# Attention plus a non-local block on one core: another order of large and small products in the q and k stages

## The chip, the cores and the metric

The kernel runs on one core of a Trainium2 chip. The metric is the device time of one execution in microseconds (us). A core has a matrix engine (TensorE, "PE" in the profile, with "PEld" for its weight loads), a vector engine (VectorE, "DVE"), a scalar engine (ScalarE, "ACT"), GpSimd ("POOL") and DMA queues. Matmul results land in PSUM, from which ACT or DVE has to read them into SBUF.

## The reference, cut to what matters

Two layers run on x, which is 8 images of 512 channels and 32 x 32 positions, in float32. The change touches only the projections q and k of the first layer.

```python
def _L0_conv_ref(x, Wq, bq, Wk, bk, Wv, bv, Wp, bp):
    q = _conv1x1(x, Wq, bq).reshape(B, h, d, H * W)     # 512x512 weights times 512x1024 data, per image
    k = _conv1x1(x, Wk, bk).reshape(B, h, d, H * W)
    v = _conv1x1(x, Wv, bv).reshape(B, h, d, H * W)
    attn = jax.nn.softmax(jnp.einsum('bhdn,bhdm->bhnm', q, k) * scale, axis=-1)
    out = jnp.einsum('bhnm,bhdm->bhdn', attn, v).reshape(B, C, H, W)
    return x + _conv1x1(out, Wp, bp)
# layer 1: theta, phi, g, a 256x256 product, the output projection, batch normalization
```

## The kernel before

Every 1x1 convolution is one step of Strassen's scheme (Winograd's form): 7 products of quarters in place of 8. The weight quarters and their sums are `w[:, 0..6]`, the data quarters are "11", "12", "21", "22" and their sums t1 to t4. In q and k, for the images 1 to 7, three of the seven products are again split into seven small products each, so that a stage has 4 large products (4 matmuls each, 128 x 512 outputs) and 3 x 7 = 21 small ones (one matmul each, 128 x 256 outputs). A float32 matmul appears in the profile as two records.

```python
SEVEN = (("11", 0, "11", 0, (("11", True),)), ("s1t1", 3, "t1", 1, (("22", True),)),
         ("s2t2", 4, "t2", 0, (("12", True),)), ("s4", 6, "22", 1, (("12", False),)),
         ("s3t3", 5, "t3", 0, (("22", False),)), ("12", 1, "21", 2, (("11", False),)),
         ("t4", 2, "t4", 0, (("21", True),)))
# (name, weight index, data, slot, (result quarter, True: write it with the bias / False: add to it))
FOUR = tuple((*one[:4], ()) for one in (SEVEN[0], SEVEN[1], SEVEN[2], FIVE[4]))
#       large products of q and k:     11 (slot 0), s1t1 (slot 1), s2t2 (slot 0), s3t3 (slot 0)
INNER = {"WqT": (1, 6, 2), "WkT": (1, 6, 2), "WpT": (1, 2)}      # which products are split again, in this order
AHEAD = {6: ((0, 0, "11", False),), 9: ((0, 0, "12", False),), 11: ((0, 1, "12", False),)}
BEHIND = {6: ((0, 1, "11", False),), 9: ((1, None, "22", True),), 11: ((1, None, "12", False),),
          15: ((0, None, "22", False), (0, None, "21", False))}
STEPS = {2: [0] * 4 + [1] * 14, 3: [0, 0, 0, 1, 2, 2, 2, 2, 1, 2, 2, 2, 2, 1, 1, 1]}
```

A large slot is a PSUM tile of two banks, one for each half m of the output rows. The three large products of slot 0 accumulate onto each other, and what stands in the slot is read out between them. `STEPS[3]` says how many small products follow each large matmul ("unit") 0 to 15. `AHEAD` and `BEHIND` say after which unit a slot (or its half m) is read, ahead of or behind the small products of that unit.

```python
def nested(name, stage, w, data, tags, first, add):              # yields one small product at a time
    slots, three = [bank(tag, f"{name}_in_{tag}") for tag in tags], len(INNER[stage]) == 3
    goes_to = {1: ("11", "21", False), 6: ("12", "22", False), 2: ("21", "t4", True)}
    for n, (q, di, begins) in enumerate(goes_to[i] for i in INNER[stage]):
        a, d = inner_blocks(w, stage, n), data[f"inner {di}"]
        pair = slots[::-1] if n % 2 else slots
        begun = set()
        for _, wi, di, s, reads in SEVEN:
            ps = pair[s % 2 if s < 2 else 1][:, s // 2, n % 2 * 256:(n % 2 + 1) * 256]
            pe(nc.tensor.matmul(ps, a[wi], d[di], start=s not in begun, stop=True, skip_group_check=True))
            begun.add(s)
            for to, is_first in reads:
                c = rows(q).start + int(to[0]) - 1
                at = cols(q).start + (int(to[1]) - 1) * 256
                (first if is_first and (begins or three) else add)((slice(c, c + 1), slice(at, at + 256)), ps)
            yield
# in seven(), inside the loop over the large matmuls:
                pe(nc.tensor.matmul(to_ps, lhsT(k), rhs(k), start=(s, at) not in begun, stop=(k == nk - 1),
                                    skip_group_check=True))
                read_parts(AHEAD.get(unit, ()))
                for _ in range(next(counts, 0)):
                    next(steps)
                read_parts(BEHIND.get(unit, ()))
                if unit in fills:
                    fills[unit]()
                unit += 1
# `first` in q and k: nc.scalar.activation(..., AF.Identity, bias=...) on ACT, one of 512 for each half, or one of 256
# `add`: nc.vector.tensor_tensor(at, at, ps, ALU.add) on DVE; pinned in program order in q, not in k
# ... cut: one image
            fills = {3: lambda: more_sums(nxt["data"], (3,), dve), 4: lambda: more_sums(nxt["data"], (4,), dve),
                     5: lambda: (of_t4.extend(inner_parts(nxt["data"], "t4", dve)), of_t4[0](), of_t4[1]()),
                     7: lambda: (of_t4[2](), of_t4[3]())}
            q, peak_q = heads_of(b + 1, "q", weights("WqT"), bq, nxt["data"], dve, inner="WqT", later=later, fills=fills)
# ... v of the next image; then k, whose gaps on DVE take the sums t1..t4 of the attention output o:
            fills = {unit: lambda i=i: more_sums(nxt["o"], (i,), dve) for unit, i in ((3, 1), (5, 2), (8, 3), (12, 4))}
```

`PE` runs strictly in the order of the program. With u for the large units and s0 to s20 for the small products, a q or k stage of before is

```
u0 u1 u2 u3 | s0 | u4 | s1 s2 | u5 | s3 s4 | u6 | s5 s6 | u7 | s7 s8 | u8 | s9 | u9 | s10 s11 |
u10 | s12 s13 | u11 | s14 s15 | u12 | s16 s17 | u13 | s18 | u14 | s19 | u15 | s20
large: u0-3 = 11, u4-7 = s1t1, u8-11 = s2t2, u12-15 = s3t3; of each four, the first two are half m = 0
small: s0-6 go to quarter 11, s7-13 to quarter 12, s14-20 to quarter 21; they use two PSUM tiles A and B by turns (s0 A, s1 B, s2 A, ...)
```

Of the kernel before, what the change touches and what calls it, by code (L numbers as in the profile page):

```python
# [30 lines left out]
def unshifted(ctx: ExitStack, tc: tile.TileContext, a: dict, out: bass.AP):  # L31
# [33 lines left out]
    dve = sp = pe  # L65
# [3 lines left out]
    def bank(tag, name):  # L69
        return psum.tile([P, 2, 512], F32, tag=tag, name=name)  # L70
# [40 lines left out]
        queue += (["WqT", "WvT", "WkT"] if b < B - 1 else []) + ["WpT", "tp", "WgT"]  # L111
    loaded = []

    INNER = {"WqT": (1, 6, 2), "WkT": (1, 6, 2), "WpT": (1, 2)}
    WIDTH = 7 * C + 3 * 3 * P
    rest = {}

# [79 lines left out]
    def more_sums(data, which, pin=lambda ins: None):  # L197
        for i in which:
            l, r = {1: ("12", "11"), 2: ("22", "t1"), 3: ("22", "12"), 4: ("21", "t2")}[i]
            data[f"t{i}"] = block(f"t{i}_{data['name']}")  # L200
            pin(nc.vector.tensor_tensor(data[f"t{i}"], data[l], data[r], ALU.subtract))
# [14 lines left out]
    def quarters_of(t):  # L216
# [13 lines left out]

    FOUR = tuple((*one[:4], ()) for one in (SEVEN[0], SEVEN[1], SEVEN[2], FIVE[4]))
    AHEAD = {6: ((0, 0, "11", False),), 9: ((0, 0, "12", False),), 11: ((0, 1, "12", False),)}
    BEHIND = {6: ((0, 1, "11", False),), 9: ((1, None, "22", True),), 11: ((1, None, "12", False),),
              15: ((0, None, "22", False), (0, None, "21", False))}
    STEPS = {2: [0] * 4 + [1] * 14, 3: [0, 0, 0, 1, 2, 2, 2, 2, 1, 2, 2, 2, 2, 1, 1, 1]}

    def nested(name, stage, w, data, tags, first, add):

        slots, three = [bank(tag, f"{name}_in_{tag}") for tag in tags], len(INNER[stage]) == 3
        goes_to = {1: ("11", "21", False), 6: ("12", "22", False), 2: ("21", "t4", True)}
        for n, (q, di, begins) in enumerate(goes_to[i] for i in INNER[stage]):
            a, d = inner_blocks(w, stage, n), data[f"inner {di}"]
# [6 lines that stand above are left out]
                for to, is_first in reads:  # L251
                    c = rows(q).start + int(to[0]) - 1
                    at = cols(q).start + (int(to[1]) - 1) * 256
                    (first if is_first and (begins or three) else add)((slice(c, c + 1), slice(at, at + 256)), ps)
                yield

    def seven(name, w, data, positions_out, first, add, between=None, early=False,
              by_chunk=False, inner=None, fills=()):

        nk, half = w.shape[2], w.shape[3]
        tags = list(free)
        free[:] = [tags[3], tags[1], tags[0], tags[2]] if early else [tags[3], tags[1], tags[2], tags[0]]
        slots, begun = {}, set()
        steps, three = iter(()), inner and len(INNER[inner]) == 3
        unit, counts = 0, iter(STEPS[len(INNER[inner])] if inner else ())
        if inner:
            free[:] = [tags[1], tags[2], tags[3], tags[0]]
            steps = nested(name, inner, w, data, tags[2:], first, add)  # L270

        def read(reads, ps):
            for to, is_first in reads:
                (first if is_first else add)(to, ps)

        def read_parts(parts):
            for s, m, to, is_first in parts if three else ():
                if m is None:
                    read(((to, is_first),), slots[s])
                else:  # L280
                    c = rows(to).start + m
                    read((((slice(c, c + 1), cols(to)), is_first),), slots[s][:, m, :])

        for n, (what, wi, di, s, reads) in enumerate(FOUR if three else FIVE if inner else EARLY if early else SEVEN):
            if s not in slots or early and what == "t4":
                slots[s] = bank(tags[s], f"{name}_{s}_{n}")
                begun -= {one for one in begun if one[0] == s}
            ps, d = slots[s], data[di]
            if positions_out:
                parts = [(ps.rearrange("p h (i f) -> p (h i) f", f=half)[:, i, :], i * half // 512,  # L290
                          lambda k, i=i: d[:, k, i * P:(i + 1) * P], lambda k: w[:, wi, k, :])
                         for i in range(512 // P)]
            else:
                parts = [(ps[:, m, :], m, lambda k, m=m: w[:, wi, k, m * P:(m + 1) * P], lambda k: d[:, k, :])
                         for m in range(half // P)]
            work = [(*part, k) for part in parts for k in range(nk)]
            if by_chunk and n == 0:
                work.sort(key=lambda one: one[4])
            for to_ps, at, lhsT, rhs, k in work:
                pe(nc.tensor.matmul(to_ps, lhsT(k), rhs(k), start=(s, at) not in begun, stop=(k == nk - 1),  # L300
                                    skip_group_check=True))
                begun.add((s, at))
                read_parts(AHEAD.get(unit, ()))
                for _ in range(next(counts, 0)):
                    next(steps)
                read_parts(BEHIND.get(unit, ()))
                if unit in fills:
                    fills[unit]()
                unit += 1
            read(reads, ps)  # L310
            if between and n in between:
                between[n]()

    def rows(q):
        return q[0] if isinstance(q[0], slice) else slice((int(q[0]) - 1) * CC // 2, int(q[0]) * CC // 2)

    def cols(q):
        return q[1] if isinstance(q[1], slice) else slice((int(q[1]) - 1) * 512, int(q[1]) * 512)
# [11 lines left out]
    _, w_first = weights_tile("WqT", C // 2)  # L330
# [474 lines left out]
    for b in range(B):  # L805
        last = b == B - 1
        nxt = {}
# [19 lines left out]
        if not last:  # L827
            inner_sums(nxt["data"], "21", dve)
            later, of_t4 = [], []
            fills = {3: lambda: more_sums(nxt["data"], (3,), dve), 4: lambda: more_sums(nxt["data"], (4,), dve),  # L830
                     5: lambda: (of_t4.extend(inner_parts(nxt["data"], "t4", dve)), of_t4[0](), of_t4[1]()),
                     7: lambda: (of_t4[2](), of_t4[3]())}
            q, peak_q = heads_of(b + 1, "q", weights("WqT"), bq, nxt["data"], dve, inner="WqT",
                                 later=later, fills=fills)
            load_w(nc.sync)

            def norm():
                nxt["products"] = normalize(denominators(next_bank(f"den_{b}")[:, 0, :]))

            v = values(b + 1, weights("WvT"), nxt["data"], {1: norm, 2: lambda: [one() for one in later], 5: lambda: nxt["products"]()})  # L840
            load_w(nc.sync)

            nxt["o"], of_21 = data_sums(quarters_of(o), f"o_{b}", ()), []
            fills = {unit: lambda i=i: more_sums(nxt["o"], (i,), dve) for unit, i in ((3, 1), (5, 2), (8, 3), (12, 4))}
            if b:
                fills[13] = lambda: (of_21.extend(inner_parts(nxt["o"], "21", dve)), of_21[0](), of_21[1]())
                fills[14] = lambda: (of_21[2](), of_21[3]())
            later_k = []
            k, peak_k = heads_of(b + 1, "k", weights("WkT"), bk, nxt["data"], later=later_k, inner="WkT",
                                 fills=fills)  # L850
            if b:
                inner_sums(nxt["o"], "t4", dve)
            load_w(nc.sync)
        else:
            nonlocal_(b - 1, held["x"], nxt["data"], held["f"], weights("WgT"), lambda: None,
                      {3: lambda: nxt.update(d=denominators(next_bank(f"den_{b}_1")[:, 0, :]))})
            z[b - 1] = [held["x"][:, cc, :] for cc in range(CC)]
            between = {4: late_unit(b - 1, 0, sums_now=False)}
            normalize(nxt["d"])()
            load_w(nc.sync)  # L860
            put_away(b - 1)
            for i, tag in enumerate("vqk"):
                reload(i, mats, tag)
            reload(3, foldp, "fold")
# [258 lines left out]
```

## Time and profile before

| | |
|---|---|
| time, median of 3 | 2166.21 us (2166.19 to 2167.51) |
| span of the profiled execution | 2164.1 us, mean granted TensorE clock 0.996 |
| one image in the steady part | 265.9 us (start of q at 721.92 to start of q at 987.80) |
| q stage | 23.62 us (987.80 to 1011.42) |
| k stage | 24.33 us (1036.80 to 1061.13) |
| DVE adds of 128x256, 128x512, 128x1024 out of PSUM | about 0.42, 0.69, 1.22 us each |
| ACT writes with bias of 128x256, 128x512 | 0.474, 0.684 us each |

The page of the profile gives each engine's busy time, the chain of work that ended last, and groups of instructions. The chain of a window, in order of time, shows for each stretch which instruction the end had to wait for: an unbroken row of PE pieces means that nothing held the matrix engine. The timeline lists one engine's instructions by their starts. The ends of matmuls are modelled, so a distance is taken from start to start.

### The profile page before, as it was taken

What the parts mean: (1) busy time and instruction counts of PE and PEld (TensorE: products, weight loads), DVE (VectorE), ACT (ScalarE), POOL (GpSimd) and SP (SyncE); (2) the same over time, 40 slices, a digit from 0 to 9 for tenths busy, and PEclk for the clock granted to TensorE, in tenths of its full rate; (3) what the DMA queues carried; (4) which work ended last, traced back from release to release, by engine and by line L of the source; (5) the groups of instructions that cost most, each with busy time, mean ns of one, the idle gap of its engine ahead of it and who ended that gap; (6) DMA issues with size and microseconds to landing.
All of it is one profiled execution on the core that took longest, in us unless ns stands there. A gap on an engine that the chain in (4) does not pass through costs nothing.

```text
span 2164.1 us, 30088 instructions
## 1 busy us (share of the span) xinstructions
PE 2133.4 (99%) x12510; PEld 1119.4 (52%) x12510; DVE 1395.0 (64%) x1634; ACT 762.1 (35%) x910; POOL 205.5 (9%) x256
## 2 busy tenths in 40 slices
PE   9999999999999999999999999999999999999996
PEld 4534664356733567335663366633666346743462
DVE  6466756667576665766657666576674675756736
ACT  1464104641046310463105621066212652056106
POOL 0111100110001100011000100011000110001000
PEclk9999999999999999999999999999999999999998
DMA  6333444333143331433323342233434234122658
GB/s 220 137 48 63 136 155 127 49 80 116 72 129 50 77 115 72 132 50 85 105 98 110 50 99 93 99 106 50 107 133 155 41 46 138 51 58 39 221 200 339
DMA packets 53375, 229.97 MB, mean 106 GB/s; under 512 B 9712, under 2 KB 16112, under 8 KB 45680
## 3 DMA queue, kind: packets, MB, share of 16 engines
q1 hardware_dynamic: 41552, 198.21, 27.2%
q0 software_dynamic: 10192, 28.46, 10.9%
q8 instruction: 100, 1.64, 0.3%
q10 hardware_dynamic: 1488, 1.32, 0.2%
q14 instruction: 43, 0.35, 0.1%
HBM read 140.79 MB, written 46.27 MB: 86 GB/s over the span
## 4 chain that ended last, share of the span: by engine, by line
PE 95%; ACT 2%; DVE 1%; DMA 1%; issue 0%; SPq 0%; DVEq 0%; ACTq 0%
PE ps L460 20%; PE po L486 20%; PE pv L300 9%; PE ptp L300 9%; PE pp L300 7%; PE pq L300 5%; PE pk L300 5%; PE pg L300 4%; PE pk_in_s L249 3%; PE pq_in_s L249 3%; PE pf L626 3%; PE pz L300 2%; PE pp_in_s L249 2%; PE pwf L661 1%; ACT z L777 1%; PE den L432 0%
## 5 line engine op out<-in xcount | busy, mean ns | idle before, releaser
L463 ACT ACTIVATE e<-ps 128x1024 f32<-128x1024 f32 x512 | 523.0, 1025 | 426.1 <-PE ps L460 420.6
L469 DVE TENSOR_TENSOR acc<-acc,e 128x1024 f32<-128x1024 f32 x384 | 470.0, 1224 | 144.3 <-ACT e L463 140.7
L486 PE MATMUL po<-e,v 64*64 64x512 f32 x4096 | 528.7, 589 | 0.7 <-ACT w_WgT L628 0.7
L460 PE MATMUL ps<-q,k 64*64 64x512 f32 x4096 | 529.1, 589 | 0.0
L486 PEld LDWEIGHTS po<-e,v 64*64 64x64 f32 x4096 | 156.4, 133 | 283.5 <-issue 275.8
L460 PEld LDWEIGHTS ps<-q,k 64*64 64x64 f32 x4096 | 155.4, 133 | 284.2 <-issue 275.1
L499 POOL DMA_DIRECT2D fold<-acc x189 | 147.1, 778 | 984.1 <-DMA fold<-acc 638.5
L467 DVE TENSOR_TENSOR acc<-e,e 128x1024 f32<-128x1024 f32 x64 | 78.3, 1224 | 144.0 <-ACT e L463 144.0
L649 ACT ACTIVATE g<-pg,gb 128x512 f32<-128x512 f32 x31 | 21.3, 688 | 374.2 <-PE pg L300 374.1
L300 PE MATMUL pv<-w_WvT,t_x 128*128 128x256 f32 x512 | 116.4, 381 | 0.0
L300 PE MATMUL ptp<-w_tp,t_x 128*128 128x256 f32 x512 | 114.4, 379 | 0.0
L300 PEld LDWEIGHTS pv<-w_WvT,t_x 128*128 128x128 f32 x512 | 96.6, 190 | 18.5 <-issue 5.7
L300 PEld LDWEIGHTS ptp<-w_tp,t_x 128*128 128x128 f32 x512 | 97.3, 190 | 13.2
L300 PE MATMUL pq<-t_x,w_WqT 128*128 128x512 f32 x200 | 101.4, 600 | 1.1 <-DVE w_WqT L788 0.8
L300 PE MATMUL pk<-t_x,w_WkT 128*128 128x512 f32 x200 | 101.5, 599 | 0.0
L300 PE MATMUL pp<-t_o,w_WpT 128*128 128x512 f32 x208 | 100.8, 592 | 0.0
L427 POOL TENSOR_SCALAR q<-q,gates 128x1024 f32<-128x1024 f32 x32 | 35.3, 1114 | 690.3 <-DVE gates L425 595.2
L415 ACT COPY v<-pv 128x1024 f32<-128x1024 f32 x32 | 32.4, 1012 | 173.2 <-PE pv L300 173.2
L300 PE MATMUL ptp<-w_tp,x 128*128 128x256 f32 x384 | 87.4, 381 | 0.0
L300 PE MATMUL pv<-w_WvT,x 128*128 128x256 f32 x384 | 86.8, 379 | 0.0
L383 ACT ACTIVATE k<-pk_in_s,bk 128x256 f32<-128x256 f32 x84 | 38.9, 474 | 116.1 <-PE pk_in_s L249 116.1
L383 ACT ACTIVATE q<-pq_in_s,bq 128x256 f32<-128x256 f32 x84 | 38.7, 474 | 115.2 <-PE pq_in_s L249 115.2
(179 smaller groups left out, 2333.6 us busy)
## 6 DMA issues: line engine op xcount, KB each, us to landing
fold<-acc POOLq DMA_DIRECT2D x189, 128.0 KB, 3.1
w_WqT<-kept_WqT SPq DMA_DIRECT2D x7, 2368.0 KB, 8.9
w_WkT<-kept_WkT SPq DMA_DIRECT2D x7, 2368.0 KB, 9.2
r<-den_d SPq DMA_DIRECT2D x32, 512.0 KB, 7.4
x<-in_x_dram SPq DMA_DIRECT2D x31, 512.0 KB, 6.3
w_WpT<-kept_WpT SPq DMA_DIRECT2D x6, 2176.0 KB, 8.4
w_WvT<-kept_WvT SPq DMA_DIRECT2D x7, 1792.0 KB, 7.1
w_tp<-kept_tp SPq DMA_DIRECT2D x7, 1792.0 KB, 7.8
```

What stands on the lines that cost most here:

```text
L249: pe(nc.tensor.matmul(ps, a[wi], d[di], start=s not in begun, stop=True, skip_group_check=True))
L300: pe(nc.tensor.matmul(to_ps, lhsT(k), rhs(k), start=(s, at) not in begun, stop=(k == nk - 1), skip_group_check=True))
L383: nc.scalar.activation(t[:, c, q[1]], ps, AF.Identity, bias=bias[:, c:c + 1])
L415: seven(f"pv_{b}", w, data, True, lambda q, ps: nc.scalar.copy(at(q), as_v(ps)), lambda q, ps: dve(nc.vector.tensor_tensor(at(q), at(q), a ...
L427: nc.gpsimd.tensor_scalar(q[:, p, :], q[:, p, :], gate[:, p:p + 1], 1.0, ALU.mult, ALU.mult)
L460: pe(nc.tensor.matmul(ps[c * P // 2:(c + 1) * P // 2, j, :], k[r, p, keys], q[r, p, h * 512:(h + 1) * 512], start=True, stop=True, skip_gr ...
L463: nc.scalar.activation(e, ps, AF.Exp, scale=SCALE)
L467: nc.vector.tensor_tensor(accs[u], es[u, 0], e, ALU.add)
L469: ins = nc.vector.tensor_tensor(accs[u], accs[u], e, ALU.add)
L486: pe(nc.tensor.matmul(ps[j * D:(j + 1) * D, r, :], v[keys, m, (2 * p + j) * D:(2 * p + j + 1) * D], e[keys, j, :], start=(m == 0), stop=(m ...
L499: nc.gpsimd.dma_start(to, part_of, accum_op=ALU.add)
L626: pe(nc.tensor.matmul(ps[:, c, :], tp[:, i, c * P:(c + 1) * P], tp[:, i, CI:], start=(i == 0), stop=(i == NB - 1)))
```

## The change

In q and k the second large product, s1t1, comes in two halves, one before and one behind the third, s2t2. A slot is now always read as a whole, and what is read of it begins a quarter of the result where it can: the reads of 11 and of 12 become writes with bias on ACT, and the small products of the quarters 11 and 12 are then all added on DVE. The small products are taken in the order quarter 11, quarter 21, quarter 12. The counts of small products behind the units 4 and 8 change from 2 and 1 to 1 and 2, and the sums on DVE that fill the gaps sit behind other units. What it is for: fewer and larger reads of the large slots, and no read of one half while the other is being written.

```diff
-    INNER = {"WqT": (1, 6, 2), "WkT": (1, 6, 2), "WpT": (1, 2)}
+    INNER = {"WqT": (1, 2, 6), "WkT": (1, 2, 6), "WpT": (1, 2)}
...
-    AHEAD = {6: ((0, 0, "11", False),), 9: ((0, 0, "12", False),), 11: ((0, 1, "12", False),)}
-    BEHIND = {6: ((0, 1, "11", False),), 9: ((1, None, "22", True),), 11: ((1, None, "12", False),),
-              15: ((0, None, "22", False), (0, None, "21", False))}
-    STEPS = {2: [0] * 4 + [1] * 14, 3: [0, 0, 0, 1, 2, 2, 2, 2, 1, 2, 2, 2, 2, 1, 1, 1]}
+    HALVES = ((0, 0), (0, 1), (1, 0), (2, 0), (2, 1), (1, 1), (3, 0), (3, 1))
+    STEPS = {2: [0] * 4 + [1] * 14, 3: [0, 0, 0, 1, 1, 2, 2, 2, 2, 2, 2, 2, 2, 1, 1, 1]}
+    READS = {3: ((0, "11", True),), 9: ((0, "12", True),), 11: ((1, "22", True), (1, "12", False)),
+             15: ((0, "22", False), (0, "21", False))}
...
-                    (first if is_first and (begins or three) else add)((slice(c, c + 1), slice(at, at + 256)), ps)
+                    (first if is_first and begins else add)((slice(c, c + 1), slice(at, at + 256)), ps)
...
-        for n, (what, wi, di, s, reads) in enumerate(FOUR if three else FIVE if inner else EARLY if early else SEVEN):
+        products = FOUR if three else FIVE if inner else EARLY if early else SEVEN
+        for n, m in HALVES if three else ((n, None) for n in range(len(products))):
+            what, wi, di, s, reads = products[n]
...
-            work = [(*part, k) for part in parts for k in range(nk)]
+            work = [(*part, k) for part in (parts if m is None else parts[m:m + 1]) for k in range(nk)]
...
-                read_parts(AHEAD.get(unit, ()))
-                for _ in range(next(counts, 0)):
-                    next(steps)
-                read_parts(BEHIND.get(unit, ()))
+                for ahead in (True, False):
+                    for one, to, is_first in READS.get(unit, ()) if three and ahead == (unit < 15) else ():
+                        read(((to, is_first),), slots[one])
+                    for _ in range(next(counts, 0) if ahead else 0):
+                        next(steps)
...
-            fills = {3: lambda: more_sums(nxt["data"], (3,), dve), 4: lambda: more_sums(nxt["data"], (4,), dve),
-                     5: lambda: (of_t4.extend(inner_parts(nxt["data"], "t4", dve)), of_t4[0](), of_t4[1]()),
-                     7: lambda: (of_t4[2](), of_t4[3]())}
+            fills = {4: lambda: more_sums(nxt["data"], (3,), dve),
+                     5: lambda: (more_sums(nxt["data"], (4,), dve), of_t4.extend(inner_parts(nxt["data"], "t4", dve))),
+                     6: lambda: (of_t4[0](), of_t4[1]()), 7: lambda: (of_t4[2](), of_t4[3]())}
...
-            fills = {unit: lambda i=i: more_sums(nxt["o"], (i,), dve) for unit, i in ((3, 1), (5, 2), (8, 3), (12, 4))}
+            fills = {unit: lambda i=i: more_sums(nxt["o"], (i,), dve) for unit, i in ((5, 1), (7, 2), (11, 3), (12, 4))}
```

The order on PE after the change, in the same notation:

```
u0 u1 u2 u3 | s0 | u4 | s1 | u5 | s2 s3 | u6 | s4 s5 | u7 | s6 s7 | u8 | s8 s9 | u9 | s10 s11 |
u10 | s12 s13 | u11 | s14 s15 | u12 | s16 s17 | u13 | s18 | u14 | s19 | u15 | s20
large: u0-3 = 11, u4-5 = s1t1 half 0, u6-9 = s2t2, u10-11 = s1t1 half 1, u12-15 = s3t3
small: s0-6 go to quarter 11, s7-13 to quarter 21, s14-20 to quarter 12; tiles A and B by turns as before
slot 0 is read whole behind u3, u9 and u15, slot 1 behind u11
```

More of the change, by code (lines that the diff above doesn't have):

```diff
@@ L233, in unshifted @@
     FOUR = tuple((*one[:4], ()) for one in (SEVEN[0], SEVEN[1], SEVEN[2], FIVE[4]))
-    AHEAD = {6: ((0, 0, "11", False),), 9: ((0, 0, "12", False),), 11: ((0, 1, "12", False),)}
-    BEHIND = {6: ((0, 1, "11", False),), 9: ((1, None, "22", True),), 11: ((1, None, "12", False),),
-              15: ((0, None, "22", False), (0, None, "21", False))}
-    STEPS = {2: [0] * 4 + [1] * 14, 3: [0, 0, 0, 1, 2, 2, 2, 2, 1, 2, 2, 2, 2, 1, 1, 1]}
+    HALVES = ((0, 0), (0, 1), (1, 0), (2, 0), (2, 1), (1, 1), (3, 0), (3, 1))
+    STEPS = {2: [0] * 4 + [1] * 14, 3: [0, 0, 0, 1, 1, 2, 2, 2, 2, 2, 2, 2, 2, 1, 1, 1]}
+    READS = {3: ((0, "11", True),), 9: ((0, "12", True),), 11: ((1, "22", True), (1, "12", False)),
+             15: ((0, "22", False), (0, "21", False))}
     def nested(name, stage, w, data, tags, first, add):
-        slots, three = [bank(tag, f"{name}_in_{tag}") for tag in tags], len(INNER[stage]) == 3
+        slots = [bank(tag, f"{name}_in_{tag}") for tag in tags]
         goes_to = {1: ("11", "21", False), 6: ("12", "22", False), 2: ("21", "t4", True)}
@@ L274, in read @@
                 (first if is_first else add)(to, ps)
[L276 to L282, printed above, removed]
-        for n, (what, wi, di, s, reads) in enumerate(FOUR if three else FIVE if inner else EARLY if early else SEVEN):
+        products = FOUR if three else FIVE if inner else EARLY if early else SEVEN
+        for n, m in HALVES if three else ((n, None) for n in range(len(products))):
+            what, wi, di, s, reads = products[n]
             if s not in slots or early and what == "t4":
```

## The prediction, made before the changed kernel was run

> **What bounds the kernel now.** First the page: busy time by engine, and the granted clock.
>
> ```profile
> span 2164.1 us, 30088 instructions
> PE 2133.4 (99%) x12510; PEld 1119.4 (52%) x12510; DVE 1395.0 (64%) x1634; ACT 762.1 (35%) x910; POOL 205.5 (9%) x256
> ...
> PEclk9999999999999999999999999999999999999998
> ```
>
> The matrix engine has work for the whole span, at full clock; DVE and ACT have a third and two thirds of theirs free. The change neither adds nor removes a matmul, so it can only win time in which PE stood still, or lose some. Busy shares cannot show that, so I read, second, the chain of work that ended last, in the window of one k stage (columns: start, length, what).
>
> ```profile
> 779.08 0.88 PE pk_in_s L249 x4
> 779.96 0.02 issue
> 779.99 0.48 ACT k L383
> 780.47 0.02 issue
> 780.49 0.04 DVE k L323
> 780.53 0.57 issue
> 781.10 0.43 DVE k L323
> 781.52 0.04 issue
> 781.57 1.13 PE pk_in_s L249 x4
> ...
> 785.71 1.11 PE pk L300 x2
> ...
> 789.41 1.11 PE pk L300 x2
> ```
>
> Undisturbed, four records of a small pair take 0.86 and two records of a large matmul 0.86 (both stand in most rows of the chain). So s7 waited from 779.94 to 781.57 and its pair then took 0.27 too long: the wait is for the DVE add of s5, which came last in DVE's queue. The two rows of 1.11 are u10 and u12, 0.25 too long each. The same view of q has no gap, only three pieces that are too long:
>
> ```profile
> 732.00 0.98 PE pq_in_s L249 x4
> ...
> 736.00 1.11 PE pq L300 x2
> ...
> 739.69 1.11 PE pq L300 x2
> ```
>
> Third, the timeline around u10 in another q stage, of which I show the DVE add, PE's weight load, its matmul and the next small one:
>
> ```profile
> 1001.12 0.69 DVE L323 TENSOR_TENSOR q<-q,pq 128x512 f32<-128x512 f32 x1 [2.17 <-PE pq L300]
> ...
> 1001.86 0.30 PEld L300 LDWEIGHTS pq<-t_x,w_WqT 128*128 128x128 f32 x2 [0.39 <-DVE q L323]
> 1001.86 1.12 PE L300 MATMUL pq<-t_x,w_WqT 128*128 128x512 f32 x2
> ...
> 1002.83 0.38 PE L249 MATMUL pq_in_s<-x,w_WqT 128*128 128x256 f32 x1
> ```
>
> The add of 1001.12 reads half 0 of slot 0; u10 writes half 1, the other bank. It still starts only 0.05 behind the add's end at 1001.81, so a write waits for every earlier read of its slot, whichever half. The load then no longer hides: u10 ends at 1002.83, 0.97 after its start instead of 0.86. So a late reader that ends at R lets PE run from R + 0.16.
>
> **What these waits cost in all.** A stage has 16 large matmuls and 21 small ones. Large: 3.43 us for the first four of k, 0.858 each; small: 0.43 each. 16 x 0.858 + 21 x 0.43 = 22.75. A k stage takes 24.33, so 1.58 is lost (1.08 at s7, 0.25 each at u10 and u12). A q stage takes 23.62; its first row is 3.63 instead of 3.43 (the turn from attention, which stays), so 0.62 to 0.67 is lost at the three places. With seven stages of each kind the most that can be won is 7 x (0.62 + 1.58) = **15.4 us**, 0.7% of 2166.2.
>
> **What the Trainium skill says.** "TensorE: Matmul & The Clock Gate", step-by-step list of Part 2: weight loads are pulled ahead, so that the next tile's load lies under the current matmul. The trace agrees: loads of 0.19 cost nothing in the rows of 0.86, and 0.11 where a wait held the load. "PSUM — Partial Sum Buffer", section on bank collisions: guard PSUM by bank. The two halves are two banks, so a guard by bank would have let u10 go; here the wait covers the whole slot, and the trace decides. "VectorE: DVE Perf Modes", section on the TRN2 errata: a fixed cost for each instruction, so small operands pay more. The trace agrees: DVE adds back to back start every 0.34, 0.59 and 1.13 us for 256, 512 and 1024 columns, which is about 0.08 plus 0.26 for each 256.
>
> **The change part by part.**
>
> *Reads.* Before, a stage has 9 small, 4 half and 3 whole adds on DVE: 9 x 0.34 + 4 x 0.59 + 3 x 1.13 = 8.8 us; after, 17 small and 3 whole: 9.2. ACT had 12 small and 2 half writes and now has 4 and 6. In a stage of 23 us neither engine becomes the bound by its sum. What counts is when each read ends.
>
> *Large slots.* Slot 0 is read by ACT behind u3 and u9. The two writes take 0.59 + 0.68 from 0.27 after the unit (an ACT or DVE read starts some 0.2 to 0.3 after the end of its product), so they end 1.54 after it. The next writers of slot 0, u6 and u12, come 3.4 and 4.3 later. Slot 1 is not written again after its read. **The waits at u10 and u12 go**: 0.5 in each stage.
>
> *Small products.* A and B alternate, so s(i+2) waits for the read of s(i). With "small, small, large" repeated there are 1.29 us between the end of s(i) and the start of s(i+2); the read needs 0.27 + 0.42 + 0.16 = 0.85. Slack: 0.44, while one of the filling sums or whole adds on DVE is 1.13. So I followed DVE's queue in its new order, times from the start of u0 (u0 held by 0.11 as in q).
>
> - DVE is busy with older work until 4.4 in q (before's t3 starts at 992.13, q at 987.73), 2.5 in k.
> - s0's add follows ACT's write: 4.54 to 4.96. s1's: 5.54 to 5.96. Then in q the sum t3 until 7.0, the adds of s2 and s3 until 7.77, t4 until 8.8, the adds of s4 and s5 until 9.24 and 9.58. The writers s2 to s7 come at 6.13, 6.56, 7.85, 8.28, 9.57, 10.00; each is free 0.1 or more earlier. The narrowest are s6, 0.17, and s7, 0.26. In k a single sum stands here (until 8.7), with the adds of s4 and s5 done by 9.15 and 9.49. **The wait at s7 goes**: 0.12 in q, 1.08 in k.
> - s8 to s13 (four of them read by ACT) have 0.4 and more, s13 0.44.
> - Behind u11 (its end 16.45) DVE starts the whole add from slot 1 at 16.72, until 17.85. s14's add comes behind it and ends at 18.27; s16 wants to start at 18.17 and gets 18.43. **A new wait of 0.26** in each stage.
> - In k two sums follow, so s16's add ends at 20.08 and s18 loses another **0.09**. In q nothing.
>
> *Sum.* q: 0.62 removed, 0.26 added: 0.36 won. k: 1.58 removed, 0.35 added: 1.23 won. 7 x (0.36 + 1.23) = **11.1 us**, so 2166.2 - 11.1 = 2155.1.
>
> **The rivals.** *All waits vanish.* If the whole add behind u11 gets behind s14's add, or a DVE read starts 0.2 instead of 0.27 after its product, the 0.26 goes: 2166.2 - 15.4 = 2150.8. For it: 0.2 is seen for some adds. Against it: in q the adds are pinned in the order of the program.
>
> *The wait moves to the chain of small adds.* Now 17 of 21 small products need DVE, and in k the adds are not pinned, so the order is open; already in the trace of before, the add of s5 lands behind two half adds that the program has one on each side of it. If a sum of 1.13 gets ahead of a waited-for add at two places in each stage, each costs 1.13 - 0.44 = 0.7, and 14 x 1.4 = 19.6 takes back the whole gain: 2166.2 - 15.4 + 19.6 = 2170. For it: the slack of 0.44 is less than one sum. Against it: PE's program order and the new places of the sums look chosen for it.
>
> *DVE hands its backlog on.* The later sums of o leave DVE busy about 4.4 us into the output projection instead of the 3.7 of before (1064.70 against its start at 1060.97). That stage has one small product between large ones and takes 23.21 against 20 x 0.858 + 14 x 0.43 = 23.18, so it waits for nothing now, and DVE idles there for 0.75 soon after. A loss of 0.5 in each of six such stages would give 2158.
>
> **Range and chances.** The lower end is the first rival, all waits gone, and a little: 2150. The upper end stands some two thirds of the way from 2155 to the second rival's 2170: 2164. Over 2% is 43 us: the gain is capped at 15.4, and a loss of that size needs 3.1 us in each of 14 stages, which only a quite different order of instructions would make. So faster by over 2%: 0.01; within 2%: 0.97; slower by over 2%: 0.02.
>
> **What would show it right or wrong.** In the chain of q and k, the rows of 1.11 at u10 and u12 and k's gap before s7 should be gone; k should take about 23.1 us and q 23.25; the pair with s16 should be some 0.26 too long, with its load waiting for a DVE add. The group of 128x256 DVE adds should grow from 63 to 119 for q and for k, and the 128x512 adds vanish there. I am wrong if PE loads wait for DVE at several small products, if the projection behind k grows past 23.21, or if k stays above 24.

## The result and the profile after

The changed kernel takes 2176.11 us (2175.83 to 2176.69) against 2166.20 for the kernel before: 9.9 us slower, ratio 1.0045 with a 95% interval of 1.0028 to 1.0062. The prediction was 2155.1, with a range of 2150 to 2164: its direction was wrong as well as its size. First the page again, busy time by engine:

```profile
span 2174.1 us, 30056 instructions
PE 2129.2 (98%) x12510; PEld 1120.5 (52%) x12510; DVE 1399.6 (64%) x1690; ACT 746.5 (34%) x854; POOL 205.1 (9%) x256
...
PEclk9999999999999999999999999999999999999998
```

The count of matmuls and the clock are as before and the span is 10 us longer, so PE now stands still more. The instruction counts moved as the prediction worked out: the group of small DVE adds is 119 for q (7 stages of 17), from 63.

```profile
L319 DVE TENSOR_TENSOR q<-q,pq_in_s 128x256 f32<-128x256 f32 x119 | 48.3, 419 | 49.1 <-PE pq_in_s L250 46.0
```

The chain of work that ended last, in a q stage (start, length, what):

```profile
735.56 0.93 PE pq_in_s L250 x4
...
741.66 0.87 PE pq L295 x2
742.53 0.02 issue
742.55 1.27 ACT q L386 x2
743.83 0.02 issue
743.85 1.23 DVE q L319
...
745.18 0.43 DVE q L319
745.61 0.04 issue
745.65 1.13 PE pq_in_s L250 x4
```

What the change was meant to remove is gone. No piece at the large units is longer than 0.87 and the old wait at s7 is 0.07 in this stage (the row of 0.93) and gone in the next (0.87); in k the row of s6 and s7 is 0.86. But s16, due at 742.53 + 0.86 + 0.86 = 744.25 (s14 and s15, then u12), starts at 745.65, and its pair takes 0.27 too long: a new wait of **1.67 us**. The chain names it link by link: u11 ends, ACT writes quarter 22 from slot 1 in two pieces, and only then does DVE's whole add from slot 1 start, then the add of s14, then s16. The timeline gives the same, with what each waited for in brackets:

```profile
742.35 0.59 PE L250 MATMUL pq_in_s<-x,w_WqT 128*128 128x256 f32 x2
...
742.55 1.27 ACT L386 ACTIVATE q<-pq,bq 128x512 f32<-128x512 f32 x2 [0.39 <-PE pq L295]
...
743.85 1.22 DVE L319 TENSOR_TENSOR q<-q,pq 128x1024 f32<-128x1024 f32 x1 [2.17 <-ACT q L386]
745.18 0.75 DVE L319 TENSOR_TENSOR q<-q,pq_in_s 128x256 f32<-128x256 f32 x2
...
745.65 0.70 PE L250 MATMUL pq_in_s<-i_x,w_WqT 128*128 128x256 f32 x2 [1.42 <-DVE q L319]
```

DVE stood idle for 2.17 us ahead of its add: it was not overloaded, it was held, at the end by ACT. In the k stage the add starts 1.32 behind u11 as well. By stage, from the chain's pieces, q went from 23.62 to 24.69 and k from 24.33 to 24.56 (one q stage of each kernel is 0.35 longer, and the first k stage went from 25.12 to 26.63). Summed over the seven of each: q 7.5, k 2.9, together 10.4 us. The spans differ by 10.0, because the last output projection got 0.48 shorter (24.62 to 24.14).

### The profile page after: what moved, and what is told of

Same layout as the page of the kernel before. It is cut to its first block, busy times and chain, and to the rows that moved or that the text cites. A ratio compares the mean times of both kernels' runs of the same rounds, so it can differ in the third digit from the quotient of the medians.

```text
span 2174.1 us, 30056 instructions
## 1 busy us (share of the span) xinstructions
PE 2129.2 (98%) x12510; PEld 1120.5 (52%) x12510; DVE 1399.6 (64%) x1690; ACT 746.5 (34%) x854; POOL 205.1 (9%) x256
## 3 DMA queue, kind: packets, MB, share of 16 engines
q10 hardware_dynamic: 1488, 1.32, 0.2%
## 4 chain that ended last, share of the span: by engine, by line
PE 94%; ACT 2%; DVE 2%; DMA 1%; issue 0%; ACTq 0%; DVEq 0%
PE ps L456 20%; PE po L482 20%; PE pv L295 9%; PE ptp L295 9%; PE pp L295 7%; PE pk L295 5%; PE pq L295 5%; PE pg L295 4%; PE pq_in_s L250 3%; PE pk_in_s L250 3%; PE pf L622 3%; PE pz L295 2%; PE pp_in_s L250 2%; PE pwf L657 1%; ACT z L773 1%; DVE k L319 1%
## 5 line engine op out<-in xcount | busy, mean ns | idle before, releaser
L319 DVE TENSOR_TENSOR q<-q,pq_in_s 128x256 f32<-128x256 f32 x119 | 48.3, 419 | 49.1 <-PE pq_in_s L250 46.0
L295 PEld LDWEIGHTS ptp<-w_tp,x 128*128 128x128 f32 x384 | 72.4, 190 | 13.0 <-issue 3.6
```

Of the source, the lines that this page charges most:

```text
L319: pin(nc.vector.tensor_tensor(at, at, ps if len(ps.shape) == 3 else ps.unsqueeze(1), ALU.add))
```

## The experiments

Theory A: the program lets no DVE read of a PSUM slot run beside an ACT read of it, so the two kinds of reads from slot 1, which the change puts side by side behind u11, run one behind the other. Theory B: 17 small adds are more than DVE can return in time, in whatever order. Theory C: DVE waits because ACT writes to the same SBUF tile, q or k.

**The add ahead of the writes.**

```diff
-             READS = {... 11: ((1, "22", True), (1, "12", False)), ...}
+             READS = {... 11: ((1, "12", False), (1, "22", True)), ...}
```

> The changed kernel with one edit: behind u11 the whole add from slot 1 (to quarter 12, on DVE) comes ahead of ACT's two writes from slot 1 (quarter 22). Theory A (DVE may not read a PSUM slot while ACT reads it, so the add waits 1.3 us for ACT's two writes and s16 waits for the add's follower): the add starts 0.2 to 0.3 us after u11 instead of 1.3, the wait at s16 shrinks from 1.68 to about 0.3 us, and the time falls by about 14 x 1.3 = 18 to 2156 to 2159 us. Theory B (17 small adds in a row are too many for DVE, whatever the order): the wait at s16 stays over 1 us and the time over 2172.

Measured: 2159.37 us (2158.95 to 2159.64), ratio to the kernel before 0.9968 (0.9955 to 0.9980). One exchange of two reads wins 16.7 us over the changed kernel. The chain in q:

```profile
737.18 0.87 PE pq L295 x2
...
738.15 1.23 DVE q L319
...
739.48 0.43 DVE q L319
739.91 0.04 issue
739.95 1.13 PE pq_in_s L250 x4
```

The timeline of the two readers:

```profile
738.15 1.22 DVE L319 TENSOR_TENSOR q<-q,pq 128x1024 f32<-128x1024 f32 x1 [0.94 <-PE pq L295]
...
739.40 1.26 ACT L386 ACTIVATE q<-pq,bq 128x512 f32<-128x512 f32 x2 [1.71 <-DVE q L319]
```

The add starts 0.10 behind u11 instead of 1.32, both by the chain, which counts from the modelled end of the product. DVE's idle time ahead of it falls from 2.17 to 0.94, and s16 loses 0.18 + 0.27 = 0.45 instead of 1.67. ACT now waits for DVE instead (its writes start at 739.40, where the add has ended), but nothing waits for ACT there. Each stage is shorter by 1.23 (q 23.46, k 23.33), and 14 x 1.23 = 17.2. Theory B falls: DVE has as many adds as in the changed kernel. The loss of 0.45 at s16 is 0.15 over the expected 0.3, and the time lies just over the expected range, for a reason told below.

**ACT's reads of slot 1 into a tile of their own.**

```diff
+                        if (one, to) == (1, "22"):
+                            first(to, data["11"])                # quarter 22 begun from a piece of x
+                            for hh in range(2):                  # slot 1 still read, into a tile nobody reads
+                                nc.scalar.activation(aside, slots[one][:, hh, :], AF.Identity, bias=...)
```

> The changed kernel, but ACT's two reads of slot 1 behind u11 write to a tile of their own that nothing reads, and quarter 22 is begun by ACT from a piece of x instead, early in the stage (so slot 1 is left out of quarter 22). Theory A (the reads of the PSUM slot exclude each other): DVE's add to quarter 12 still starts only about 1.3 us after u11, and the time stays within 3 us of 2176. Theory C (the add waits because ACT writes the same SBUF tile q or k): the add starts 0.2 to 0.3 us after u11 and the time falls to about 2158.

Measured: 10151.44 us. This kernel leaves slot 1 out of quarter 22, and the piece of x made q and k so large that the kernel's bound on the scores sent it through its second branch too, so its time can't be compared. Its q stages, ahead of that branch, already show the add only when ACT has done (ACT's reads from 743.73, the add at 745.16). The next run takes the second branch away.

> As the run with the aside tile, but ACT begins quarter 22 early with the bias alone (the piece of x times zero), so that q and k stay small and only the first branch of the kernel runs; slot 1 is still left out of quarter 22, and ACT still reads slot 1 behind u11, into a tile that nothing reads. Theory A (reads of one PSUM slot exclude each other): DVE's add to quarter 12 starts about 1.3 us after u11, the wait at s16 is about 1.7 us, the time 2173 to 2179. Theory C (the wait comes from ACT's write to q or k): the add starts 0.1 to 0.3 us after u11, the time is 2158 to 2162.

```diff
-                            first(to, data["11"])
+                            first(to, data["11"], 0.0)           # scale 0: the bias alone
```

Measured: 2179.26 us (one run; the kernel before beside it 2166.40). That is just over the expected 2173 to 2179. The timeline of DVE and ACT:

```profile
743.43 1.41 ACT L306 ACTIVATE aside<-pq,bq 128x512 bf16<-128x512 f32 x2 [0.39 <-PE pq L295]
...
744.88 1.22 DVE L325 TENSOR_TENSOR q<-q,pq 128x1024 f32<-128x1024 f32 x1 [2.31 <-ACT aside L306]
```

ACT's writes to quarter 22 were over at 726.5, so at this point ACT and DVE share nothing but slot 1, which both only read, and the add still waits until ACT is done, 1.45 behind the start of its first read. Theory C falls. (A stage takes 0.1 to 0.2 more than in the changed kernel: ACT's two writes to the one small tile take 1.41 instead of 1.27.)

Nor do ACT and DVE keep apart whenever both read PSUM. In the changed kernel, behind u9, a DVE add from the small tiles and an ACT write from slot 0 run side by side:

```profile
739.61 0.78 DVE L319 TENSOR_TENSOR q<-q,pq_in_s 128x256 f32<-128x256 f32 x2 [2.18 <-PE pq_in_s L250]
739.69 0.68 ACT L386 ACTIVATE q<-pq,bq 128x512 f32<-128x512 f32 x1
```

It is the common tile that makes one wait for the other.

**The add cut in halves, one bank each.**

```diff
+                        if (one, to) == (1, "12"):
+                            for hh in range(2):
+                                c = rows(to).start + hh
+                                read((((slice(c, c + 1), cols(to)), False),), slots[one][:, hh, :])
+                            continue
```

> The changed kernel with the add from slot 1 cut in two halves, each reading one bank of the slot; ACT's two writes stay ahead and read one bank each. If reads exclude each other bank by bank: the first half add starts about 0.9 us after u11, when ACT is done with its first half, and the wait at s16 shrinks by about 0.5 us, the time by 5 to 8 us. If they exclude each other by the whole slot, as the writes before did: the first half add starts 1.3 us after u11 as the whole add did, and the time stays within 2 us of 2176.

Measured: 2174.62 us (one run), within the 2 us expected for the whole slot. The timeline:

```profile
742.74 1.26 ACT L391 ACTIVATE q<-pq,bq 128x512 f32<-128x512 f32 x2 [0.39 <-PE pq L295]
...
744.03 1.29 DVE L324 TENSOR_TENSOR q<-q,pq 128x512 f32<-128x512 f32 x2 [2.17 <-ACT q L391]
```

The first half add reads only bank 0, which ACT finishes with at about 743.4, and it starts at 744.03, when both of ACT's reads are over. So this program keeps the two readers apart by slot (the tile), not by bank.

**The add behind the adds of s14 and s15, and the sums of o moved.**

```diff
-             READS = {... 11: ((1, "22", True), (1, "12", False)), ...}
+             READS = {... 11: ((1, "22", True),), ...}
+    BACK = {11: ((1, "12", False),)}                             # read behind the small products of the unit
-    ... for unit, i in ((5, 1), (7, 2), (11, 3), (12, 4))}      # k: sums t1..t4 of o
+    ... for unit, i in ((5, 1), (7, 2), (8, 3), (9, 4))}
```

> The changed kernel with the whole add from slot 1 placed behind the adds of s14 and s15, ACT's writes from slot 1 left where they are, and in k the third and fourth sum of o behind the units 8 and 9 instead of 11 and 12. Theory A: s16 finds the add of s14 done, no wait of over 0.1 us is left in q or k of the images 2 to 7, each stage takes about 22.9 us (q) and 22.8 (k), and the time is 2150 to 2154 us, 12 to 16 below the kernel before. Theory B: waits at s16 or s18 of 0.3 us or more stay, and the time is over 2160.

Measured: 2152.66 us (2152.33 to 2153.09), ratio to the kernel before 0.9936 (0.9919 to 0.9952): faster than both. A q stage takes 23.05, a k stage 22.85, and the chain in k has only PE pieces, of which the one with s18 is 0.05 too long:

```profile
786.22 0.86 PE pk_in_s L251 x4
787.08 0.86 PE pk L296 x2
787.94 0.48 PE pk_in_s L251 x2
788.42 0.86 PE pk L296 x2
```

Here ACT and DVE still read slot 1 one behind the other, but no product waits for the second reader. The waits that the prediction hoped to win are won: 13.6 of the 15.4.

**The same with the sums left where they were.** Only the `BACK` part of the edit above; the sums stay behind the units 11 and 12.

> The kernel with the add behind s14 and s15, but with the sums of o in k left behind the units 11 and 12. If the place of the add alone does it: q stays at 23.05 us and k at 22.85, the time at 2152 to 2154. If the sums matter as well: in k the third sum stands between the whole add and the add of s16, s18 waits 0.5 to 0.9 us more, k takes 23.4 to 23.8, q 23.05, and the time is 2156 to 2159.

Measured: 2159.06 us (2158.86 to 2159.90), ratio 0.9967 (0.9955 to 0.9980). q is 23.05 to 23.06 as in the run above, k 23.79 instead of 22.85. Against the changed kernel, the place of the add is worth all that q won (24.69 to 23.05) and 0.77 in k (24.56 to 23.79); the place of the sums is worth the other 0.94 in k, 7 x 0.94 = 6.6 us. The timeline of DVE in k shows why:

```profile
787.35 1.22 DVE L322 TENSOR_TENSOR k<-k,pk 128x1024 f32<-128x1024 f32 x1
788.49 1.22 DVE L201 TENSOR_TENSOR t_o<-o 128x1024 f32<-128x1024 f32 x1
789.62 0.94 DVE L322 TENSOR_TENSOR k<-k,pk_in_s 128x256 f32<-128x256 f32 x2
```

The whole add and a sum stand in a row; the adds behind them, s16's first, start at 789.62, and s18 waits for that one.

**The kernel before, with half 0 read later.** This tests what the prediction said of u10 and u12.

```diff
-    AHEAD = {6: ((0, 0, "11", False),), 9: ((0, 0, "12", False),), 11: ((0, 1, "12", False),)}
+    AHEAD = {6: ((0, 0, "11", False),), 11: ((0, 0, "12", False), (0, 1, "12", False))}
```

> The kernel before with one edit: half 0 of slot 0 is read into quarter 12 behind u11, together with half 1, instead of behind u9. If a write waits for every earlier read of its slot, whichever half: u10 (half 1) waits no more, its piece of the chain falls from 1.11 to 0.86 us, and u12 waits for two half adds instead of one, 0.8 to 0.9 us instead of 0.25; the time rises by about 14 x 0.35 = 5 us to 2171. If u10 waited for something else, its piece stays at 1.11.

Measured: 2168.62 us (one run), 2.2 above the kernel before beside it; I expected 5. A k stage takes 24.61, which is 0.28 more and not 0.35. The chain in k:

```profile
786.96 0.86 PE pk L300 x2
787.81 0.86 PE pk_in_s L249 x4
788.68 0.87 PE pk L300 x2
789.55 0.02 issue
789.57 1.30 DVE k L323 x2
790.87 0.04 issue
790.91 1.13 PE pk L300 x2
```

The piece of u10 (the first row) falls to 0.86 and u12 now loses 0.78: a matmul into half 1 did wait for the read of half 0. That part of the prediction stands.

**The sums of Wp pinned.** On top of the fastest kernel so far, for the first k stage, which stays at 25.06.

```diff
-                weight_sums(w, corner[name])
+                weight_sums(w, corner[name], dve if name == "WpT" else lambda ins: None)     # dve: pinned in program order
```

> The kernel with the add behind s14 and s15 and the sums of o moved, plus one edit: the four DVE sums of the weights Wp, made once beside the first k stage, are pinned in program order behind the fills of that stage. If these sums, standing between the adds of s0 and s1, are what makes the first k stage 25.06 us where the others take 22.85 (0.81 of it are the small bias products): the first k stage falls by about 1 to 1.4 us, the others stay, the time is 2151 to 2152. If not, it stays at 25.06.

Measured: 2151.76 us (2151.38 to 2151.99), ratio to the kernel before 0.9933 (0.9916 to 0.9949), the fastest of all. The first k stage falls from 25.06 to 24.11, by 0.95 and so a little under the expected 1 to 1.4; the others stay. What is left of its excess stands at its end:

```profile
259.87 0.02 issue
259.89 1.56 DVE k L322 x2
```

The output projection starts only behind these adds, at 261.50. In the kernel before, where the last small product was read by ACT, no such row stands there.

## Why the prediction was wrong, by its own steps

- *The bound and the cap* were right: PE at full clock, no matmul added or removed. With the collision out of the way, and the sums moved, 13.6 us of the 15.4 came; with the sums of Wp pinned as well, 14.6.
- *"The waits at u10 and u12 go", "The wait at s7 goes"*: right, by the chain above. So the gain was there in the changed kernel too, some 15 us of it.
- *The step that failed* stands in the part on small products: "Behind u11 (its end 16.45) DVE starts the whole add from slot 1 at 16.72". It counted only the end of the product as a condition. The prediction takes u11's end where s14 starts, and puts the add 0.27 behind that. The add started 1.50 behind s14 (743.85 against 742.35), because ACT's two writes read the same slot ahead of it; with the add ahead of the writes it started 0.27 behind (738.15 against 737.88). I followed DVE's queue and ACT's queue each by itself and never asked whether they meet in one slot. The wait of 0.26 at s16 became 1.67. The exchange of the two reads prices this: 1.23 us in each stage, 17.2 in all.
- *A second, smaller mis-sizing in the same step*: the add of s14 was put 1.13 behind the whole add's start, the distance of DVE adds back to back. But s14 adds to the quarter which the whole add has just written, so it waits for its end: 739.48 - 738.15 = 1.33. That is 0.20 a stage, 2.8 us; with the 1.3 of the first k stage (next point) the exchanged order comes to 2155.1 + 2.8 + 1.3 = 2159.2, against 2159.37 measured.
- *The sum with the right terms*: the prediction's 23.25 and 23.1 for q and k, plus 1.23 and 0.20, give 24.68 and 24.53; measured 24.69 and 24.56. The first k stage lost 1.3 more than the others (26.63 less the 0.81 of its bias products is 25.82, against 24.56); there the sums of Wp got between the adds of s0 and s1, which with the change both run on DVE. The run with these sums pinned takes 0.95 of such a loss out of the fastest kernel; the rest is the wait of the output projection behind that stage.
- *The rivals*: "All waits vanish" named the cure, the whole add behind s14's add, at 2150.8; built, with the sums of o moved too, it took 2152.66. "The wait moves to the chain of small adds" named the right place and the right size of time (2170), but for another reason, a filling sum ahead of an add; it was weighed as the upper end of things, and the range stopped short of it. The sums do cost, 6.6 us in k once the add stands behind s15. "DVE hands its backlog on" did not happen: the projection behind k takes 23.21 as before.
- The Trainium skill could have warned. "PSUM — Partial Sum Buffer", section on bank collisions, says that two engines must not be in one bank at the same time, reads against reads included. I took from that section only the writes of PE against readers. The runs agree in that ACT's and DVE's reads of slot 1 never overlap, but the program keeps apart whole slots of two banks. No run here shows what the chip would have done without that wait.

## What to carry to other kernels

When two engines are to read one PSUM tile in a program that keeps its readers apart as this one does, treat them as one queue: count the second reader from the end of the first, and let the reader for whom a product waits go first, or place the add that nobody waits for behind those that somebody does. Follow each product back through every queue that touches its tile, and where an add builds on what its own engine has just written, count from that one's end.

## What the runs showed that was not expected

- In this program ACT's and DVE's reads of one PSUM tile run one behind the other, though they write to different places and touch different banks: the first half add waited 0.6 us for ACT's read of the other bank.
- Behind a whole add, a DVE add that builds on what it wrote starts 1.33 us behind its start (743.85 to 745.18), an independent one (the sum of o at 788.49 behind the add at 787.35) 1.14 behind.
